# Attention units in rounds of five with borrowed PSUM banks, and queries loaded two chunks ahead

## The chip, the cores and the metric

The kernel runs on one core of a Trainium2 chip. The metric is the device time of one execution in microseconds (us), the median over runs. Engines are named as the profile names them: PE multiplies matrices (PEld loads its weights), DVE and ACT work on vectors, POOL is the general engine, SP issues most of the DMAs.

## What is computed

The reference normalises an input of 2048 tokens by 512 features and adds two branches to it. The first is differential attention: 16 heads, each with two softmax maps of depth 16 over one 32-wide value, causal; the difference of the two maps is filtered along the tokens (an FFT with a Gaussian), normalised and projected. The second is a mixture of experts: every token goes through a shared expert and through the best 2 of 8 routed experts.

```python
s = einsum('bthd,bshd->bhts', q, k) * scale
a = softmax(where(causal, s, NEG))          # for q1,k1 and for q2,k2
o = concat([a @ v1, a @ v2])
attn = irfft((rfft(attn1) - lambda_full * rfft(attn2)) * filt) # then rms norm, @ Wout
y = sum_k topk_w[k] * expert_k(x) + shared(x)
out = x + attn_branch(layernorm(x)) + ffn_branch(layernorm(x))
```

## The kernel before, in words

Three stages follow each other: a beginning (normalise, route, project queries and keys, store them in DRAM), the function `middle` (attention and experts interleaved), and `ending` (filter, output projection, and the gathering of the experts' rows). The change is in `middle`, which holds PE from 254.0 us to about 1221 us of the profiled execution.

The attention is cut into 32 **chunks**: 8 groups `g` of two heads, and in each group four blocks of 512 queries, `qc` = 3, 2, 1, 0. A chunk is a list of **units** (`Chunk.units`). A unit is one head and one block of 128 keys (`kb`): both softmax maps of that head against 512 queries. Units on the diagonal are narrower, and two of them share one; these are called masked. A chunk has 8 qc + 5 units, so there are 68 in a group and 544 in all. `LEAD` says how many whole key blocks come ahead of the diagonal.

`scores` (L831) works a unit off: two matmuls side by side, each on 64 rows of the array (maps s = 0 and 1), into the two halves of a PSUM tile `ps_s`; ACT takes the exponential of both halves in one instruction (L844) into `pt`; POOL zeroes the masked triangles (L853). Later `values` (L875) multiplies `pt` with the values, four matmuls side by side of 32 columns, into `ps_o`; DVE adds `pt` up into `sum` (L889, L892), which `sums` (L901) and `finish` (L913 to L930) turn into the divisor.

PSUM has eight banks here. `sc_ps` has 2 tiles of two banks, `av_ps` one bank, and `f_ps` three banks, handed out by `bank`, which the experts' products use (`wh` L244, `wy` L283, `ps_x` L167, `xh` and `xg` L181, `ps_u` L204, `xy` L214), and the chunk's ends too (`ps_sum`, `ps_ot`, `ps_st`).

The order of the work on PE is written out in the main loop at the end of `middle`, one **round** for every four units of the stream: scores of the first two units; the value products that are pending (`todo`), and the sums of a chunk that ended in the round before (`closing`); scores of the other two units; the remaining value products; then `work()`, one or more pieces of the experts, until their share of the work done has caught up with the share of the stream. `added` puts DVE's sums between the pieces. At the end of a round POOL may get up to two steps of `folded`, which prepares the filter for a finished group.

When a chunk's first unit comes up, `burst` issues loads on SP's queue: `load_queries` of the next chunk (8 DMAs of 64 KB, two buffers for each head), and `load_keys` of the next group for the block of keys that this group has done with (4 DMAs of 128 KB). The experts' weights go over the same queue (`fetch`, L151: 704 or 768 KB each), issued by the pieces of the experts as buffers come free. Six of the last eight of the 34 routed tiles hold two experts of 64 tokens each, and fetch two sets of weights for a tile.

Of the kernel before, what the change touches and what calls it, by code (L numbers as in the profile page):

```python
# [8 lines left out]
F32 = mybir.dt.float32  # L9
F32R = mybir.dt.float32r  # L10
BF16 = mybir.dt.bfloat16
I32 = mybir.dt.int32
AF = mybir.ActivationFunctionType
# [57 lines left out]
def block_kernel(  # L71
# [521 lines left out]
    def middle(general):  # L593


        with ExitStack() as pools:
# [130 lines left out]

            def load_keys(g, c):
                for h in (2 * g, 2 * g + 1):
                    k = kp.tile([P, QC], F32R, tag=f"k{c}", name="kS", bufs=4 if c == 0 else 2)  # L730
                    for s in range(2):
                        src = parts[1][2 * h + s, :, :, c * QC : (c + 1) * QC].rearrange("a d t -> (a d) t")
                        nc.sync.dma_start(
                            k[64 * s : 64 * s + 64, :].bitcast(F32),
                            src.unsqueeze(0).to_broadcast([2, 2 * D, QC]),
                        )
                    keys[h, c] = k

            def load_queries(g, qc):
                for h in (2 * g, 2 * g + 1):  # L740
                    q = qp.tile([P, QC], F32R, tag=f"q{h % 2}", name="qS")
                    for s in range(2):
                        for rep in range(2):
                            r = 64 * s + 32 * rep
                            nc.sync.dma_start(
                                q[r : r + 32, :].bitcast(F32),
                                parts[0][2 * h + s, rep : rep + 2, :, qc * QC : (qc + 1) * QC].rearrange("a d t -> (a d) t"),
                            )
                    queries[h, qc] = q
# [45 lines left out]
            def masked(chunk, unit):  # L795
                return any(kb >= chunk.qc * TQ for _, kb, *_ in unit)

            class Chunk:
# [6 lines left out]
                def units(self):  # L805


                    d = self.qc * TQ
                    for kb in [*range(LEAD[self.qc]), d]:
                        for h in range(2):  # L810
                            yield [(h, kb, 0, 0, QC)]
                    for h in range(2):
                        yield [(h, d + 1, P, 0, 3 * P), (h, d + 3, 3 * P, 3 * P, P)]
                    last = [(h, d + 2, 2 * P, 2 * P * h, 2 * P) for h in range(2)]
                    yield from ([part] for part in last) if general else [last]
                    for kb in range(LEAD[self.qc], d):
                        for h in range(2):
                            yield [(h, kb, 0, 0, QC)]

                def scores(self, unit):  # L820

                    g, qc = self.g, self.qc
                    if general and not self.probs:
                        self.shift = greatest(g, qc)
                    ps = sps.tile([P, 2, QC], F32, tag="sc", name="ps_s")
                    for h, kb, off, col, w in unit:
                        for s in range(2):
                            r = slice(64 * s, 64 * s + 64)
                            k = keys[2 * g + h, kb // TQ][r, kb % TQ * P : (kb % TQ + 1) * P]
                            to = ps[:, s, col : col + w]  # L830
                            nc.tensor.matmul(  # L831
                                to, k, queries[2 * g + h, qc][r, off : off + w], start=True, stop=not general
                            )
                            if general:
                                r = 64 * h + 32 * s
                                nc.tensor.matmul(
                                    to, ones[r : r + 1, :], self.shift[r : r + 1, off : off + w],
                                    start=False, stop=kb < qc * TQ,
                                )
                                if kb >= qc * TQ:  # L840
                                    nc.tensor.matmul(to[:, :P], identb, mask, start=False, stop=True)
                    pt = pp.tile([P, 2, QC], F32, tag="pt", name="pt")
                    used = slice(min(c for *_, c, _ in unit), max(c + w for *_, c, w in unit))
                    nc.scalar.activation(pt[:, :, used], ps[:, :, used], AF.Exp, scale=SCALE)  # L844
                    if masked(self, unit) and not general:

                        cols = [col for *_, col, _ in unit]
                        if cols == [0, 2 * P]:
                            chosen = [pt.rearrange("p s (h q) -> p (s h) q", h=2)[:, :, :P]]
                        else:  # L850
                            chosen = [pt[:, :, col : col + P] for col in cols]
                        for part in chosen:
                            nc.gpsimd.affine_select(  # L853
                                out=part, in_=part, pattern=[[0, part.shape[1]], [1, P]], compare_op=ALU.is_ge,
                                fill=0.0, base=0, channel_multiplier=-1,
                            )
                    ready = []
                    for h, kb, off, col, w in unit:
                        self.probs[h, kb] = pt[:, :, col : col + w], off
                        if (1 - h, kb) in self.probs:  # L860
                            ready.append((self, kb))
                    return ready
# [133 lines left out]
            ex = experts()  # L996
            for c in range(NQC):
                load_keys(0, c)
                if c == 0:
                    load_queries(0, NQC - 1)  # L1000
            worked, begun, summed, held = 0.0, -1, 0, []
            todo, closing, closed, shared, ready, folding = [], [], [], [], [], None

            def burst(units):
                nonlocal begun
                found = []
                for n, chunk, unit in units:
                    if n > begun:
                        begun = n
                        if n + 1 < len(turns):  # L1010
                            load_queries(*turns[n + 1])

                        if chunk.g + 1 < NG:
                            load_keys(chunk.g + 1, (chunk.qc + 1) % NQC)
                    found += chunk.scores(unit)
                return found

            def values():
# [16 lines left out]
                    else:  # L1035
                        held.append((n, c, unit))

            for i in range(0, len(stream), 4):
                units = stream[i : i + 4]
                found = burst(units[:2])  # L1040
                n, ended = values()
                for c in closing:
                    c.sums()
                    summed += 1
                if n < 2 and not closing:

                    work()
                found += burst(units[2:])
                while todo:
                    ended += values()[1]  # L1050
                todo += found
                for c in closed:
                    c.put(nc.gpsimd)
                    if c.qc == 0:
                        ready.append(c.g)
                closed, closing = closing, ended
                for c in closed:
                    c.finish()
                held, before = [], held
                added(before)  # L1060
                added(units[:2])
                later = [u for u in units[2:] if not masked(*u[1:])]
                while True:
                    work()
                    added(later[:1])
                    later = later[1:]
                    if worked / (work_all - left) >= (i + 4) / len(stream):
                        break
                added(later)
                added(u for u in units[2:] if masked(*u[1:]))  # L1070
                if any(masked(*u[1:]) for u in units) or not shared:
                    steps = 0
                elif any(masked(*u[1:]) for u in stream[i + 4 : i + 8]):
                    steps = 1 if ready or units[0][1].g == NG - 1 else 0
                else:
                    steps = 2
                for _ in range(steps):
                    if folding is None and ready:
                        folding = folded(ready.pop(0), nc.gpsimd)
                    if folding is not None and next(folding, 0) == 0:  # L1080
                        folding = None
# [401 lines left out]
```

## Time and profile before

| what | value |
|---|---|
| median of 3 runs | 1334.18 us (1333.29 to 1334.27) |
| profiled execution, its own time | 1336.14 us |
| its span, first to last instruction | 1334.3 us |
| PE busy | 1305.5 us, 98% of the span |
| DVE, ACT, POOL busy | 1007.7, 690.5, 620.3 us |
| scores L831, matmuls and busy | 1280, 204.5 us |
| values L875, matmuls and busy | 2560, 267.7 us |
| exponentials L844 | 544, 1022 ns each |
| granted PE clock, mean | 0.996 |

A row of the timeline gives the start of a group of equal instructions, how long it lasted, the engine, the line, what is written from what, rows by columns of the array, and how many there were; square brackets show idle time of the engine ahead of it and what ended it. The lasting of matmuls overlaps, so differences of starts are what counts. An fp32 product takes two matmuls of the trace where the program has one.

### The profile page before, as it was taken

How to read it: one execution, taken by the hardware profiler on the slowest of the kernel's cores; microseconds unless marked ns; L12 is line 12 of the kernel's file. 1: busy time of each engine (PE TensorE's matmuls, PEld its weight loads, DVE VectorE, ACT ScalarE, POOL GpSimd, SP SyncE). 2: the span in 40 equal slices, each digit the busy share in tenths (PEclk: the TensorE clock that was granted, in tenths of full speed). 3: DMA queues.
4: the chain of work that ended last, by engine and by line, in shares of the span. 5: the costliest groups of instructions: out<-in, count | busy, mean ns of one | idle time of the engine just before them, and what ended most of it. 6: DMA issues, size and time to landing. Idle time of an engine off the chain costs nothing.

```text
span 1334.3 us, 20914 instructions
## 1 busy us (share of the span) xinstructions
PE 1305.5 (98%) x7554; PEld 598.5 (45%) x7554; DVE 1007.7 (76%) x1316; ACT 690.5 (52%) x848; POOL 620.3 (46%) x639
## 2 busy tenths in 40 slices
PE   7999999999999999999999999999999999999998
PEld 3444444434343444444445444444544443445544
DVE  7049883277777868778987988888798869876784
ACT  2311110265666566666666666666666657662231
POOL 0002331012131233215985976894598666741774
PEclk9999999999999999999999999999999999999999
DMA  9405773201210023235566666566666667878998
GB/s 371 184 16 163 201 205 102 89 16 32 66 63 22 29 78 93 77 111 160 169 186 202 183 196 188 149 215 191 170 199 189 191 186 271 314 266 304 190 222 188
DMA packets 82058, 215.07 MB, mean 161 GB/s; under 512 B 12964, under 2 KB 13416, under 8 KB 81688
## 3 DMA queue, kind: packets, MB, share of 16 engines
q1 hardware_dynamic: 69224, 186.47, 43.9%
q0 software_dynamic: 11056, 22.78, 8.7%
q10 hardware_dynamic: 1664, 4.38, 1.0%
q8 instruction: 63, 1.03, 0.4%
q14 instruction: 51, 0.42, 0.1%
HBM read 170.48 MB, written 43.10 MB: 160 GB/s over the span
## 4 chain that ended last, share of the span: by engine, by line
PE 64%; POOL 8%; DMA 5%; issue 2%; DVE 2%; ACT 0%; SPq 0%; POOLq 0%; DVEq 0%; ACTq 0%
PE ps_o L875 17%; PE ps_s L831 12%; PE wh L244 8%; PE xy L214 6%; PE xh L181 5%; PE xg L181 5%; PE wy L283 4%; POOL res L1138 3%; DMA res<-ysh 2%; PE ps_sum L901 2%; DMA w<-in_wex_dram 1%; PE ps_x L167 1%; POOL pt L853 1%; DVE sum L892 1%; PE ps_ot L913 1%
## 5 line engine op out<-in xcount | busy, mean ns | idle before, releaser
L892 DVE TENSOR_TENSOR sum<-sum,pt 128x1024 f32<-128x1024 f32 (+2 forms) x576 | 628.7, 1140 | 30.4 <-POOL pt L853 13.6
L844 ACT ACTIVATE pt<-ps_s 128x1024 f32<-128x1024 f32 x544 | 527.3, 1022 | 182.5 <-PE ps_s L831 127.3
L853 POOL TENSOR_SCALAR_AFFINE_SELECT pt<-pt 128x256 f32<-128x256 f32 (+1 forms) x224 | 164.4, 756 | 368.4 <-ACT pt L844 342.9
L875 PE MATMUL ps_o<-pt,vd 128*32 128x512 f32 (+3 forms) x2560 | 267.7, 534 | 1.9 <-POOL pt L853 1.9
L831 PE MATMUL ps_s<-qS,kS 64*128 64x512 f32 (+3 forms) x1280 | 204.5, 407 | 1.6 <-DVEq L1346 1.2
L831 PEld LDWEIGHTS ps_s<-qS,kS 64*128 64x128 f32 x1280 | 97.5, 185 | 177.3 <-issue 96.7
L244 PE MATMUL wh<-xnT,w 128*128 128x512 f32 (+1 forms) x352 | 150.4, 574 | 0.0
L875 PEld LDWEIGHTS ps_o<-pt,vd 128*32 128x32 f32 x2560 | 67.2, 109 | 123.3 <-issue 105.9
L495 POOL DMA_INDIRECT who<-pairs,slot x32 | 33.8, 1055 | 171.3 <-DVE pairs L492 104.3
L542 PE MATMUL ps_x<-xnT,wqk_sb 128*128 128x512 f32 x256 | 110.5, 593 | 0.0
L244 PEld LDWEIGHTS wh<-xnT,w 128*128 128x128 f32 x352 | 64.1, 190 | 72.6 <-issue 56.5
L214 PE MATMUL xy<-w,uT 128*128 128x512 f32 (+3 forms) x240 | 94.6, 599 | 1.2 <-DVE rcp L916 1.2
L181 PE MATMUL xh<-w,xT 128*128 128x352 f32 (+1 forms) x320 | 90.4, 477 | 4.0 <-DMA w<-in_wex_dram 3.2
L181 PE MATMUL xg<-w,xT 128*128 128x352 f32 (+1 forms) x320 | 88.6, 468 | 0.0
L930 POOL TENSOR_TENSOR vd<-o_n 128x128 f32<-128x128 f32 x60 | 58.1, 986 | 53.8 <-DVE o_n L921 53.7
L542 PEld LDWEIGHTS ps_x<-xnT,wqk_sb 128*128 128x128 f32 x256 | 48.4, 190 | 60.6 <-issue 60.6
L283 PE MATMUL wy<-w,ws 128*128 128x512 f32 x160 | 74.8, 603 | 0.0
L559 ACT CAST hi<-turned 128x1024 fp32r<-128x1024 f32 x16 | 16.7, 1045 | 93.9 <-DVE turned L557 59.3
L1138 POOL DMA_INDIRECT res<-ys,slot x32 | 53.3, 1667 | 23.7 <-DMA res<-ysh 11.7
L181 PEld LDWEIGHTS xh<-w,xT 128*128 128x128 f32 (+1 forms) x320 | 48.3, 178 | 31.0 <-issue 9.3
L181 PEld LDWEIGHTS xg<-w,xT 128*128 128x128 f32 (+1 forms) x320 | 46.6, 174 | 34.4 <-issue 14.8
L377 PE MATMUL ps_tv<-wv_sb,xnT 128*128 128x512 f32 x128 | 59.8, 620 | 0.7 <-ACT xnT L374 0.7
(252 smaller groups left out, 1368.4 us busy)
## 6 DMA issues: line engine op xcount, KB each, us to landing
w<-in_wex_dram SPq DMA_DIRECT2D x88, 704.0 KB
w<-in_wex_dram SPq DMA_DIRECT2D x44, 768.0 KB
kS<-parts_k SPq DMA_DIRECT2D x128, 128.0 KB
qS<-parts_q SPq DMA_DIRECT2D x256, 64.0 KB
ys<-y_sb SPq DMA_DIRECT2D x34, 256.0 KB
parts_q<-hi SPq DMA_DIRECT2D x32, 256.0 KB
parts_k<-hi SPq DMA_DIRECT2D x16, 256.0 KB
parts_k<-turned SPq DMA_DIRECT2D x16, 256.0 KB
```

Source lines behind the costliest of these rows:

```text
L181: nc.tensor.matmul(dst[r, :], xT[:, c, r], w[:, c * FI : (c + 1) * FI], start=(c == 0), stop=(c == NE - 1), skip_group_check=True,)
L214: nc.tensor.matmul(y[r, :], uT[:m, ic, r], w[:m, ic * E : (ic + 1) * E], start=(ic == 0), stop=(ic == NF - 1), skip_group_check=True,)
L244: nc.tensor.matmul(dst, w_sb[o // WUP][o % WUP // WONE][:, o % WONE : o % WONE + P], x[:, c, :], start=(c == 0), stop=(c == NE - 1),)
L283: nc.tensor.matmul(y, us[i][:, t * P : (t + 1) * P], w_sb[i // NF][2][:, i % NF * E : (i % NF + 1) * E], start=(i == 0), stop=(i == SCH - 1),)
L377: nc.tensor.matmul(pv, xnT[:, c, t * P : (t + 1) * P], wv_sb[:, c, :], start=(c == 0), stop=(c == NE - 1))
L542: nc.tensor.matmul(ps[:, i, :], wqk_sb[st, qk][:, i, c, :], xnT[:, c, cols], start=(c == 0), stop=(c == NE - 1),)
L831: nc.tensor.matmul(to, k, queries[2 * g + h, qc][r, off : off + w], start=True, stop=not general)
L844: nc.scalar.activation(pt[:, :, used], ps[:, :, used], AF.Exp, scale=SCALE)
L853: nc.gpsimd.affine_select(out=part, in_=part, pattern=[[0, part.shape[1]], [1, P]], compare_op=ALU.is_ge, fill=0.0, base=0, channel_multip ...
L875: nc.tensor.matmul(self.o[r : r + 32, off:], vd[:, kb, v0 : v0 + 32], pt[:, s, :], start=first, stop=self.ended, skip_group_check=True,)
L892: nc.vector.tensor_add(to, to, pt)
L1138: nc.gpsimd.indirect_dma_start(out=came[k], out_offset=None, in_=ys, in_offset=bass.IndirectOffsetOnAxis(ap=slot[:, step - 2, order[k] : o ...
```

## The change

- A round takes 5 units where no chunk ended in the round before (`closing` is empty), else 4. The second burst of such a round has three units, and the first of them (`apart`) puts its scores in two banks from `f_ps` (`ps_a`) in the place of a `ps_s` tile. Its exponential is two instructions of 512 columns.
- Queries have three buffers for each head, and are loaded two chunks ahead: `load_queries(*turns[n + 2])`, and the first two chunks' before the loop, the second of them between the keys of block 1 and block 2.
- The keys of block 0 have two buffers, not four. They are loaded when their own group begins, not a group ahead; so the chunk `qc` = 3 takes its key blocks 4 to 15 first and 0 to 3 last.
- POOL's steps of `folded` in a round: one if the round's units hold no masked one, one more if the next four hold none.

```diff
-                    k = kp.tile([P, QC], F32R, tag=f"k{c}", name="kS", bufs=4 if c == 0 else 2)
+                    k = kp.tile([P, QC], F32R, tag=f"k{c}", name="kS")
...
-                    q = qp.tile([P, QC], F32R, tag=f"q{h % 2}", name="qS")
+                    q = qp.tile([P, QC], F32R, tag=f"q{h % 2}", name="qS", bufs=3)
...
-                    for kb in [*range(LEAD[self.qc]), d]:
+                    kbs = [*range(TQ, d), *range(TQ)] if self.qc == NQC - 1 else [*range(d)]
+                    for kb in [*kbs[: LEAD[self.qc]], d]:
...
-                    for kb in range(LEAD[self.qc], d):
+                    for kb in kbs[LEAD[self.qc] :]:
...
-                def scores(self, unit):
+                def scores(self, unit, apart):
...
-                    ps = sps.tile([P, 2, QC], F32, tag="sc", name="ps_s")
+                    if apart:
+                        banks = [bank([P, QC], "ps_a") for _ in range(2)]
+                    else:
+                        ps = sps.tile([P, 2, QC], F32, tag="sc", name="ps_s")
+                        banks = [ps[:, s] for s in range(2)]
...
-                            to = ps[:, s, col : col + w]
+                            to = banks[s][:, col : col + w]
...
-                    nc.scalar.activation(pt[:, :, used], ps[:, :, used], AF.Exp, scale=SCALE)
+                    if apart:
+                        for s in range(2):
+                            nc.scalar.activation(pt[:, s, used], banks[s][:, used], AF.Exp, scale=SCALE)
+                    else:
+                        nc.scalar.activation(pt[:, :, used], ps[:, :, used], AF.Exp, scale=SCALE)
...
-                if c == 0:
-                    load_queries(0, NQC - 1)
+                if c < 2:
+                    load_queries(0, NQC - 1 - c)
...
-                        if n + 1 < len(turns):
-                            load_queries(*turns[n + 1])
-
-                        if chunk.g + 1 < NG:
-                            load_keys(chunk.g + 1, (chunk.qc + 1) % NQC)
-                    found += chunk.scores(unit)
+                        if n + 2 < len(turns):
+                            load_queries(*turns[n + 2])
+
+                        c = (chunk.qc + 1) % NQC
+                        g = chunk.g + (c > 0)
+                        if 0 < g < NG:
+                            load_keys(g, c)
+                    found += chunk.scores(unit, k == len(units) - 3)
...
-            for i in range(0, len(stream), 4):
-                units = stream[i : i + 4]
+            upto = 0
+            while upto < len(stream):
+
+                many = 4 if general or closing else 5
+                units = stream[upto : upto + many]
+                upto += many
...
-                    if worked / (work_all - left) >= (i + 4) / len(stream):
+                    if worked / (work_all - left) >= upto / len(stream):
...
-                if any(masked(*u[1:]) for u in units) or not shared:
-                    steps = 0
-                elif any(masked(*u[1:]) for u in stream[i + 4 : i + 8]):
-                    steps = 1 if ready or units[0][1].g == NG - 1 else 0
-                else:
-                    steps = 2
-                for _ in range(steps):
+                steps = [
+                    shared and not any(masked(*u[1:]) for u in some) for some in (units, stream[upto : upto + 4])
+                ]
+                for _ in range(sum(map(bool, steps))):
```

## Prediction

> **What bounds the kernel now.** I read the page's busy shares and its chain first.
>
> ```profile
> PE 1305.5 (98%) x7554; PEld 598.5 (45%) x7554; DVE 1007.7 (76%) x1316; ACT 690.5 (52%) x848; POOL 620.3 (46%) x639
> PE 64%; POOL 8%; DMA 5%; issue 2%; DVE 2%; ACT 0%; SPq 0%; POOLq 0%; DVEq 0%; ACTq 0%
> ```
>
> PE is the bound of the span and, in `middle`, of nearly every stretch; the POOL and DMA shares of the chain lie mostly after 1221 us, in the ending, which the change doesn't edit and which starts when `middle` is done. So time can be won in `middle` only if PE needs less of it, or waits less. No matmul goes away. The timeline of PE shows what can: how long a group holds PE depends on what is beside it.
>
> ```profile
> 242.32 4.45 PE L283 MATMUL wy<-w,ws 128*128 128x512 f32 x10
> ...
> 246.61 1.02 PE L283 MATMUL wy<-w,u_last 128*128 128x512 f32 x2
> ...
> 415.71 3.70 PE L244 MATMUL wh<-xnT,w 128*128 128x512 f32 x8
> 419.34 0.73 PE L831 MATMUL ps_s<-qS,kS 64*128 64x512 f32 x4
> 420.00 1.92 PE L875 MATMUL ps_o<-pt,vd 128*32 128x512 f32 x16
> 421.85 0.73 PE L831 MATMUL ps_s<-qS,kS 64*128 64x512 f32 x4
> 422.52 2.84 PE L244 MATMUL wh<-xnT,w 128*128 128x512 f32 x6
> ```
>
> From start to start, ten full-array matmuls in an unbroken run take 246.61 - 242.32 = 4.29 us, 0.429 each. Eight of them between scores take 419.34 - 415.71 = 3.63 us, where 8 x 0.429 = 3.43: **0.20 us of switching for each stay in the experts' form**. Sixteen value matmuls, four side by side, take 421.85 - 420.00 = 1.85, where 4 x 0.429 = 1.72: 0.138 us (unrounded starts) for each stay in the values' form. Two units of scores cost 0.66 after either. In the starts of single matmuls the 0.20 splits into 0.105 on the way in and 0.093 on the way out, the 0.138 into 0.024 and 0.114. These repeat to a few ns over the whole stage.
>
> Then PE's waits and what was behind the largest:
>
> ```profile
> PE xh L181 <- DMA w<-in_wex_dram: 3.2, 2, 2.1
> PE ps_o L875 <- POOL pt L853: 1.9, 3, 1.4
> PE xy L214 <- DVE rcp L916: 1.2, 1, 1.2
> ```
>
> SP's queue, and PE at the wait:
>
> ```profile
> 1068.75 7.43 SPq L745 DMA_DIRECT2D qS<-parts_q  x8
> 1076.22 2.38 SPq L733 DMA_DIRECT2D kS<-parts_k  x4
> 1079.99 3.89 SPq L151 DMA_DIRECT2D w<-in_wex_dram  x4
> ```
>
> ```profile
> 1094.84 0.78 PE L181 MATMUL xh<-w,xT 128*64 128x352 f32 x2 [2.08 <-DMA w<-in_wex_dram]
> 1096.69 4.96 PE L181 MATMUL xh<-w,xT 128*64 128x352 f32 x14 [1.07 <-DMA w<-in_wex_dram]
> ```
>
> And the stretch after it (PE, PEld, DVE, ACT and POOL busy with counts, PE clock, DMA share, GB/s):
>
> ```profile
> 1095.00:1103.00 8.00, 6.93 (x24) 2.36 (x27) 2.67 (x5) 1.03 (x2) 5.15 (x5) 0.57 0.50 140
> ```
>
> At 1092 us PE waits for the second two-expert tile's weights, which stood behind a chunk's loads on SP. After it the granted clock is 0.57 over 1095 to 1103 (the trace has half clock for 6.83 us). The episode costs 2.08 + 1.07 us idle and half of 6.83: 6.5 us. Such waits in `middle` sum to about 14 us, this one the largest.
>
> **The change part by part.** *Rounds of five.* I counted stays in the order of PE's instructions in both built programs, from the first score to the last value product: 84 rounds of five and 31 of four in place of 136 of four; stays in the experts' form (128 rows, transposes of a chunk's end included) 155 before, 127 after; stays in the values' form 153 before, 134 after. So 28 x 0.198 + 19 x 0.138 = 5.5 + 2.6 = **8.2 us less on PE**. The third unit in a burst costs what a unit costs: start to start the pairs of scores take 0.32 to 0.33 us in either place. The switch costs lie on the path, as PE has no slack here; from below the saving is bounded at nothing, if each switch removed is found again as a wait.
>
> By the Trainium skill, page "TensorEngine Tiling (Array Packing)", section "Key Properties", a change of tiling mode drains the array; "TensorE: Matmul & The Clock Gate", section "Part 2", in "Single matmul latency", puts a drain at about 175 ns. Two switches for each of the 47 stays would then be an estimate of 16 us, or 1318; the starts above show 24 to 114 ns a switch, so the measurement decides.
>
> *The borrowed banks.* The third unit no longer waits for the first's exponential. What is new: two of the three expert banks are held until ACT has read them. Take a round as in the timeline, from its first score at 0: values end at 2.5, the three units at 3.5. ACT does a 1024-column exponential every 0.92 us (row: 1022 ns, overlapping), so the first two end at 2.4, the borrowed two at about 3.5 and 4.0, the last two by 5.9. The expert's first product starts at 3.5 in the third bank; its second, where a round has a short product first (`ps_u` or `ps_x`, 0.48 us), at 4.0 in the first borrowed bank: ready by half a microsecond. The next round's first two scores come no earlier than 3.5 + 2.56 = 6.1 and 6.4, and want the tiles free at 5.0 and 5.9: covered, but by 0.5 us for the second. Splitting an exponential costs ACT between 0.04 (at the 0.48 us pitch of its 512-column copies) and 0.26 us (two unoverlapped 592 ns instructions) a round: at most 22 us, on an engine that is free for 640. I take 0 for PE, and as the other end 0.1 us in each of 84 rounds, 8.4 us.
>
> *Masks on POOL.* A round of five may hold a whole diagonal: seven selections at 0.76 us. Before, the widest selection of each chunk ended 0.56 to 5.9 us ahead of its value product, median 3.6; the distance on PE between that score and that product is 5.2 to 8.6 us before and 5.3 to 11.3 after. Steps of `folded` ahead of masked rounds stay one or two of some 5 us. No leftover step is at the end. I take 0; the ends are -1.9 (the row's waits gone) and +4.
>
> *The loads.* Query and key loads keep their number and size, at the same chunk starts. At the start, eight query loads come ahead of the keys of blocks 2 and 3. SP took from 215.5 to 227.3 for eight, so the last keys go out near 258 and land near 264; the first unit that wants them stands in the third round, after 254 + 19 = 273. Hidden, with 9 us to spare. Late, the last group's first chunk now brings four key loads (0.5 MB) that the kernel before had sent a group earlier; they stand behind the weights of the second two-expert tile and ahead of that tile's successor. The earlier queries take a risk away: the eight that SP reached at 1083.9 took 16.7 us to go out, and now have a chunk more of time. For the wait at 1092 itself: after, the loads of chunk (6, 0) stand one weight fetch further ahead of the tile's, but the distance on PE from that chunk's start to the tile, summed from the rows' durations along each built order, is 21.5 us, where it was 21.4. So I take the episode as unchanged; the ends are -6.5 (gone) and +6.5 for each further one.
>
> By the page "TensorE: Matmul & The Clock Gate", section "Why this matters for your kernels", idle gaps under some 3 us keep the clock. The row above speaks against it: the longest gap before the half clock was 2.08 us. By the rule that part, 3.4 us, would not be there to lose.
>
> **Sum.** The profiled execution took 1336.14 for a span of 1334.3, and 1336.14 - 8.2 = 1327.9. It stands 2.0 above the median of 1334.18; taken off the median, 8.2 gives **1326.0**.
>
> **Rivals.** *A, the weights come in time:* the fetch of the second double tile is behind fewer bytes in flight. 8.2 + 6.5 less: 1319.5. For it, DMA was only 18% busy at 1075 to 1080 while SP stood in front of its query slots; against it, the equal distance.
>
> *B, the saving is eaten in small waits:* 0.1 us for banks in each round of five, 8.4 us, or masks at 0.26 us in each of 32 chunks. 1334. For it, covers of half a microsecond; against it, scores started later than their usual distance by under 3 us in all of the 136 rounds.
>
> *C, slower:* one mechanism, weights late on SP in the stretch of double tiles (1070 to 1200 us), each time with the half clock after it. Price 6.5 us each; two more than now give 1334.2 - 8.2 + 13 = 1339. It makes the kernel slower from 1.7 of them on ((8.2 + 2.7) / 6.5). For it, DMA at 0.8 to 0.9 there and 0.5 MB of keys added; against it, only one in the six double tiles before.
>
> *D, it doesn't do what it says* is out: the built order shows the rounds and stays counted above.
>
> **How the numbers follow.** Forecast 52% (1322.5 to 1329.5 of its own: POOL and the smaller waits -3.5 to +3.5), A 20%, B 16%, C 12%. About 0.2%, 2.7 us, is what a measurement of this kernel can tell from no change. Faster: forecast, A and a third of B that ends below 1331.5, 0.77; same: the rest of B, 0.11; slower: 0.12. The range leaves out C and A's best: 1317 to 1334.
>
> **What would show it.** PE's timeline should show scores in groups of six, value groups of 24, and stays still 0.20 and 0.138 us over their matmuls; PE busy near 1297. Wrong if PE's idle list gains `ps_a`, `xh` or `xy` behind ACT, or `ps_o` behind POOL, over 3 us; if the clock shows a second half-clock stretch; or none, which is A.

## The result and the profile after

The changed kernel takes **1407.64 us** (median of 4, 1405.58 to 1408.99) beside 1333.74 us for the kernel before (median of 4): a ratio of 1.0553, with a 95% interval of 1.0534 to 1.0571. It is slower by 5.5%, where 1326.0 was forecast. The profiled execution took 1407.89 us for a span of 1406.2, against 1336.14 and 1334.3 before; its mean granted clock is 0.971, against 0.996.

The first view is again the page of the changed kernel: its busy shares, the row of the granted PE clock in 40 slices (in tenths, 9 is 90% or more), and the chain by engine.

```profile
PE 1315.9 (94%) x7554; PEld 612.5 (44%) x7554; DVE 1011.3 (72%) x1316; ACT 694.5 (49%) x932; POOL 615.8 (44%) x639
...
PEclk9999999999899999999998999799889989999999
...
PE 56%; DMA 11%; POOL 9%; issue 3%; DVE 2%; SPq 1%; ACT 1%; POOLq 0%; DVEq 0%; ACTq 0%
```

PE has the same 7554 instructions and is busy 10 us longer, not 8 us shorter. Its share of the chain has gone from 64% to 56%, and DMA's from 5% to 11%. The clock has dips at regular distances. The kernel before had none in its row:

```profile
PEclk9999999999999999999999999999999999999999
```

PE's waits in the changed kernel (waiting tile and line, releaser, us in total, times, longest):

```profile
PE ps_s L838 <- DMA kS<-parts_k: 51.0, 16, 6.4
...
PE ps_s L838 <- issue: 6.7, 2, 3.7
PE xh L181 <- DVE rcp L927: 2.6, 1, 2.6
...
PE ps_u L204 <- DVE xtanh L198: 1.8, 1, 1.8
...
PE xy L214 <- DMA w<-in_wex_dram: 1.6, 1, 1.6
PE ps_o L886 <- POOL pt L864: 1.4, 4, 0.5
PE ps_a L838 <- DMA kS<-parts_k: 1.3, 1, 1.3
```

The first row is new and is the result: scores wait 51 us for **keys**, and the "issue" row (6.7) is of the same places, as the timeline below shows. The wait for weights that the prediction dwelt on is 1.6 us here. The seven places are the starts of groups 1 to 7: by the starts of the trace 10.3 us at 366, 3.9 at 500, 1.6 at 617, 7.2 at 740, 13.1 at 872, 13.0 at 1007 and 10.5 at 1143 us, 59.7 together before rounding.

One of them in full. SP's queue around the sixth, in the changed kernel:

```profile
988.75 12.19 SPq L151 DMA_DIRECT2D w<-in_wex_dram  x3
1000.98 7.75 SPq L745 DMA_DIRECT2D qS<-parts_q  x8
1008.78 2.27 SPq L733 DMA_DIRECT2D kS<-parts_k  x4
...
1013.08 12.59 SPq L745 DMA_DIRECT2D qS<-parts_q  x8
```

PE there, and the stretch as a whole (busy PE, PEld, DVE, ACT and POOL with counts, PE clock, DMA share, GB/s):

```profile
1004.53 2.74 PE L214 MATMUL xy<-w,uT 128*128 128x512 f32 x6
1013.69 0.76 PE L838 MATMUL ps_s<-qS,kS 64*128 64x512 f32 x1 [6.42 <-DMA kS<-parts_k]
1016.35 0.79 PE L838 MATMUL ps_s<-qS,kS 64*128 64x512 f32 x1 [1.89 <-DMA kS<-parts_k]
1020.09 0.76 PE L838 MATMUL ps_s<-qS,kS 64*128 64x512 f32 x1 [2.95 <-issue]
1022.64 0.79 PE L838 MATMUL ps_s<-qS,kS 64*128 64x512 f32 x1 [1.79 <-DMA kS<-parts_k]
1023.36 4.18 PE L886 MATMUL ps_o<-pt,vd 128*32 128x512 f32 x32
```

```profile
1007.00:1027.00 20.00, 6.95 (x33) 2.52 (x36) 4.27 (x6) 2.79 (x4) 3.93 (x5) 0.58 0.41 115
```

The four key loads leave SP at 1008.78, behind eight query loads that took 7.75 us to go out; PE has stood since 1007.3. It gets one matmul per landed load until 1022.6. Which keys are they? Of the **next** group, block 1 (`kb` 4 to 7). They are issued when the chunk `qc` = 0 begins, five units ahead of the next group. In the kernel before, the chunk `qc` = 3 began with `kb` 0 to 3, whose keys had been loaded a group earlier, and wanted `kb` 4 with its 9th unit. The changed one begins with `kb` 4, so that the same load, issued at the same point, is wanted eight units sooner. Around it the clock is 0.58: after the seven stops the trace records 78.5 us at half clock (13.65, 3.41, 3.41, 10.24, 17.07, 17.07 and 13.65), and in all of `middle` 81.9: another 3.41 follow the 2.6 us that `xh` waits behind `rcp`.

**A ledger.** The starts of the trace allow a sum for `middle`. Each stay of PE in one form lasts from its first start to the next stay's first start; take off its matmuls at their unbroken pace, and the median of what is left is the price of a stay. What stands over 0.15 us above that price is a wait or half clock. Kernel before: 17.7 us of such excess; changed kernel: 105.6. The stays became fewer, 106.5 us before and 89.8 now. So 87.9 - 16.7 = 71.2 us more, against 71.9 between the two spans. The forecast failed by the first number; the second is twice what it gave.

### The profile page after: what moved, and what is told of

It reads as the page before. It is cut to its first block, busy times and chain, and to the rows that moved or that the text cites. A ratio compares the mean times of both kernels' runs of the same rounds, so it can differ in the third digit from the quotient of the medians.

```text
span 1406.2 us, 20962 instructions
## 1 busy us (share of the span) xinstructions
PE 1315.9 (94%) x7554; PEld 612.5 (44%) x7554; DVE 1011.3 (72%) x1316; ACT 694.5 (49%) x932; POOL 615.8 (44%) x639
## 4 chain that ended last, share of the span: by engine, by line
PE 56%; DMA 11%; POOL 9%; issue 3%; DVE 2%; SPq 1%; ACT 1%; POOLq 0%; DVEq 0%; ACTq 0%
PE ps_o L886 15%; PE ps_s L838 8%; PE wh L244 8%; DMA kS<-parts_k 6%; PE xh L181 5%; PE xy L214 5%; PE xg L181 5%; PE wy L283 3%; POOL res L1152 2%; PE ps_a L838 2%; DMA w<-in_wex_dram 2%; PE ps_sum L912 2%; DMA res<-ysh 2%; POOL pt L864 2%; PE ps_ot L924 1%
## 5 line engine op out<-in xcount | busy, mean ns | idle before, releaser
L855 ACT ACTIVATE pt<-ps_s 128x1024 f32<-128x1024 f32 x460 | 447.3, 1028 | 169.2 <-PE ps_s L838 130.3
L864 POOL TENSOR_SCALAR_AFFINE_SELECT pt<-pt 128x256 f32<-128x256 f32 (+1 forms) x224 | 183.5, 845 | 353.7 <-ACT pt L855 272.1
L886 PE MATMUL ps_o<-pt,vd 128*32 128x512 f32 (+3 forms) x2560 | 270.8, 546 | 1.5 <-POOL pt L864 1.4
L838 PE MATMUL ps_s<-qS,kS 64*128 64x512 f32 (+3 forms) x1082 | 174.9, 396 | 59.7 <-DMA kS<-parts_k 51.0
L838 PEld LDWEIGHTS ps_s<-qS,kS 64*128 64x128 f32 x1082 | 90.5, 186 | 151.1 <-issue 106.5
L853 ACT ACTIVATE pt<-ps_a 128x512 f32<-128x512 f32 x168 | 91.6, 596 | 54.5 <-PE ps_a L838 37.6
L941 POOL TENSOR_TENSOR vd<-o_n 128x128 f32<-128x128 f32 x60 | 49.7, 848 | 136.7 <-DVE o_n L932 136.7
L927 DVE RECIPROCAL rcp<-ps_st 128x16 f32<-128x16 f32 x32 | 8.2, 255 | 106.7 <-PE ps_st L925 106.7
```

Of the source, the lines that this page charges most:

```text
L838: nc.tensor.matmul(to, k, queries[2 * g + h, qc][r, off : off + w], start=True, stop=not general)
L853: nc.scalar.activation(pt[:, s, used], banks[s][:, used], AF.Exp, scale=SCALE)
L864: nc.gpsimd.affine_select(out=part, in_=part, pattern=[[0, part.shape[1]], [1, P]], compare_op=ALU.is_ge, fill=0.0, base=0, channel_multip ...
L886: nc.tensor.matmul(self.o[r : r + 32, off:], vd[:, kb, v0 : v0 + 32], pt[:, s, :], start=first, stop=self.ended, skip_group_check=True,)
```

## The experiments

Theory K: the order of the key blocks makes the first scores of groups 1 to 7 wait for loads; nothing else in the change costs much. Rivals: the rounds of five, which use keys up faster (F), and the loads' traffic, whose effect is on the weights (L). The "excess" given with each run is the ledger's, for its `middle`.

**a_order: the changed kernel with the key blocks 8 to 11 first.** These are loaded two chunks ahead of the group; `kb` 4 is again wanted with the 9th unit.

```diff
-  kbs = [*range(TQ, d), *range(TQ)] if self.qc == NQC - 1 else [*range(d)]
+  kbs = [*range(2 * TQ, d), *range(TQ, 2 * TQ), *range(TQ)] if self.qc == NQC - 1 else [*range(d)]
```

> The changed kernel with one line other: the chunk qc = 3 takes key blocks 8 to 11, then 4 to 7, then 0 to 3 (with its lead of six and the diagonal as before), in the place of 4 to 11, then 0 to 3. Theory (keys too late): the loss is that block 1's keys go out when chunk (g, 0) begins, five units ahead of the chunk that now starts with them; here they are wanted eight whole units later, so the waits of scores on kS (about 60 us in the changed kernel) fall under 3 us, the half-clock stretches at the groups' beginnings go, and the time is that of the 8.2 us saved: 1326 (1320 to 1332). Rival 1 (queue overfull: two chunks of queries ahead, and block 0's keys at a group's start, make all keys late): waits on kS stay over 30 us, 1370 to 1410. Rival 2 (rounds of five themselves stall PE): 1370 to 1410 with waits on ACT.

Measured: 1339.04 us (8 runs), ratio 1.0027 (1.0017 to 1.0038); clock 0.992, excess 33.8. Its largest waits of PE in `middle`:

```profile
PE xy L214 <- DMA w<-in_wex_dram: 7.9, 1, 7.9
...
PE xh L181 <- DMA w<-in_wex_dram: 3.1, 2, 2.2
PE xh L181 <- DVE rcp L927: 3.1, 2, 2.6
PE xh L181 <- ACT xT L169: 2.5, 1, 2.5
```

Scores wait for no keys any more: one line gives 69 of the 74 us back. But the time lies above the range of K (1320 to 1332), as the kernel is not the 8 us faster that was forecast. A wait for weights of 7.9 us with 10.24 us at half clock has come, and waits of 2.5, 1.8 and 2.65 us at 597, 612 and 742 us.

**b_order: the kernel before with the changed order of key blocks alone.**

```diff
-  for kb in [*range(LEAD[self.qc]), d]:
+  kbs = [*range(TQ, d), *range(TQ)] if self.qc == NQC - 1 else [*range(d)]
+  for kb in [*kbs[: LEAD[self.qc]], d]:
...
-  for kb in range(LEAD[self.qc], d):
+  for kb in kbs[LEAD[self.qc] :]:
```

> The kernel before with the changed kernel's order of key blocks in chunk qc = 3 alone (4 to 11, then 0 to 3); rounds of four, loads, buffers as before. Theory (keys too late): the whole loss and nothing of the gain: waits on kS of about 60 us, half clock for about 80 us in all, 1334 + 75 to 85, so 1409 to 1419. Rival 1 (queue overfull): no loss without the other loads, 1334. Rival 2 (rounds of five): 1334.

Measured: 1417.22 us, ratio 1.0603 (1.0584 to 1.0622); clock 0.970, excess 100.5. The first waits of PE:

```profile
PE ps_s L832 <- DMA kS<-parts_k: 44.2, 17, 4.7
PE ps_s L832 <- issue: 9.5, 4, 3.0
PE ps_s L832 <- DMA w<-in_wex_dram: 7.6, 2, 4.1
```

All three rows are scores of the first units of a group. Three lines in the kernel before, without rounds of five and without queries two chunks ahead, cost 82 us. So the order of the key blocks is the cause, shown from both sides; whether the rest of the change is free, the other half of K, is asked further down.

**a_four: the changed kernel with rounds of four.**

```diff
-  found += chunk.scores(unit, k == len(units) - 3)
+  found += chunk.scores(unit, False)
...
-  many = 4 if general or closing else 5
+  many = 4
```

> The changed kernel with rounds of four throughout, so without the borrowed banks; order of keys, loads and buffers as changed. Theory (keys too late): the loss without the gain, 1405 to 1420. Rival 1 (queue overfull): the same, 1405 to 1420. Rival 2 (rounds of five): 1334.

Measured: 1424.47 us, ratio 1.0660 (1.0642 to 1.0677); excess 109.5. It lies 4 us above K's range. Without the rounds of five the kernel is 17 us slower still: F is out as the cause, and the rounds are worth about twice the forecast's 8.2.

**b_five: the kernel before with the rounds of five alone**, banks and split exponential as in the change, loads and key order as before.

```diff
-  for i in range(0, len(stream), 4):
-      units = stream[i : i + 4]
+  upto = 0
+  while upto < len(stream):
+      many = 4 if general or closing else 5
+      units = stream[upto : upto + many]
+      upto += many
...
+  if apart:
+      banks = [bank([P, QC], "ps_a") for _ in range(2)]
```

> The kernel before with rounds of five and the borrowed banks alone; order of key blocks, loads, buffers and the rule for POOL's steps as before. Theory (keys too late; the rounds save what was counted): 1334 - 8 = 1326, scores never waiting for kS. Rival 1: 1326 as well. Rival 2 (rounds of five stall PE): 1370 to 1410. Of the prediction's own rivals: if banks or masks eat the saving, 1334.

Measured: 1334.09 us (10 runs), ratio 0.9987 (0.9977 to 0.9997); excess 31.0. The 1326 of the expectation did not come. The saving on the stays is there and nearly eaten, by the same waits at 597, 611 and 741 us, by 4.5 us for weights at 1089, and by 1.9 us for queries and 1.2 for keys at 956. The time is that of the rival "banks or masks", but none of these waits is for a borrowed bank or a mask. The one at 741 us is for another bank: `xh` reads only weights and ACT's copy `xT`, so what it waits for behind DVE's `rcp` can only be its bank of `f_ps`, which a chunk's end (`ps_st`) holds until then.

**a_keys: the changed kernel with the key loads issued ahead of the queries'.** A smaller dose of the same delay.

```diff
+  c = (chunk.qc + 1) % NQC
+  g = chunk.g + (c > 0)
+  if 0 < g < NG:
+      load_keys(g, c)
   if n + 2 < len(turns):
       load_queries(*turns[n + 2])
-
-  c = (chunk.qc + 1) % NQC
-  g = chunk.g + (c > 0)
-  if 0 < g < NG:
-      load_keys(g, c)
```

> The changed kernel with each chunk's key loads put ahead of its query loads on SP; order of key blocks as changed (4 to 11 first). Theory (keys too late, by the time from issue to first use): SP took 7.75 us for the eight query loads in front of the keys at 1001 us, so each group's wait on kS shrinks by about that. The seven groups' waits were 10.3, 3.9, 1.6, 7.2, 13.1, 13.0 and 10.5 us; less 7.75 each, not below 0, they leave 16 of 60 us. With less half clock: 1345 to 1370. Rival (total traffic makes keys late, wherever they stand): as changed, 1400 to 1412.

Measured: 1368.59 us in one run only (before: 1334.83, median of 17), excess 64.7; the waits for keys are 20.2 us in place of 51.0. The place in SP's queue is more than half of the cost; five units are too short for the loads even without the queries ahead.

**a_both: both, the order of a_order and the queue of a_keys.**

> The changed kernel with both edits: key blocks 8 to 11, 4 to 7, 0 to 3 in chunk qc = 3, and each chunk's keys loaded ahead of its queries. Theory: keys were in time already with the order alone, so this does what the order alone does, 1336 to 1341 beside 1335 before; the 7.9 us wait for a weight of the experts at 1104 us stays, since as many loads stand ahead of that weight on SP. Rival (keys that are only just in time hold small waits): 1330 or less.

Measured: 1332.94 us (10 runs), ratio 0.9984 (0.9973 to 0.9994), excess 30.0: below the theory's range and above the rival's, so neither had it. The wait for weights near 1101 us stays, with 5.5 us and 6.83 us at half clock. Which load is ahead of which among a chunk's own does not free the weights.

**a_order4: a_order with rounds of four** (the edit of a_four). It asks whether that wait is brought by the rounds or by the loads.

> The kernel with the mended order (8 to 11, 4 to 7, 0 to 3) and the changed loads, in rounds of four. It tells what ate the 8.2 us in the mended order. Theory L (the loads: block 0's keys now go out at the group's start, and hold the weights of the double tiles up on SP): the 7.9 us wait with its half clock stays, 1343 to 1350. Theory R (the rounds of five are what brings the new waits, on weights too): 1333 to 1337, no wait for a weight over 3 us.

Measured: 1355.69 us, ratio 1.0156 (1.0141 to 1.0171), excess 34.5; it is above L's range (1343 to 1350). Its waits of PE on experts' operands:

```profile
PE xy L214 <- DMA w<-in_wex_dram: 6.7, 1, 6.7
PE xy L214 <- DVE rcp L927: 4.9, 2, 3.1
PE xh L181 <- DMA w<-in_wex_dram: 4.1, 2, 3.0
```

The weights are late with rounds of four too, so L holds for that part: the changed loads delay them. The waits of 2.5 and 1.8 us at 597 and 611 are gone (0.7 is left for the copy), so those belong to the rounds of five. The pair a_order and a_order4 gives the rounds' worth again: 15.8 us between the profiled executions (1336.91 and 1352.74); L's range was too low since it went by 8.2. And the second half of K falls: with the keys in time and rounds of four, the rest of the change still costs 21 us beside the kernel before.

What L means can be read from SP's queue in a_order. The wait on PE was from 1103.7 to 1111.59.

```profile
1078.17 14.63 SPq L745 DMA_DIRECT2D qS<-parts_q  x8
1092.84 2.37 SPq L733 DMA_DIRECT2D kS<-parts_k  x4
...
1097.04 4.51 SPq L151 DMA_DIRECT2D w<-in_wex_dram  x5
```

The chunks `qc` = 0 and the next `qc` = 3 begin only five units apart, and each sends eight query loads and four key loads. The second's queries took 14.63 us to leave SP, and the five weight loads behind them went out from 1097.04 on. But neither those queries (wanted two chunks on) nor the keys of block 0 (now wanted last) are urgent.

**a_late: a_both, where a chunk `qc` = 3 of a later group sends its key loads with its 7th unit and its query loads with its 13th.**

```diff
-  if n > begun:
-      begun = n
+  late = chunk.qc == NQC - 1 and chunk.g > 0 and not general
+  seen[n] = seen.get(n, 0) + 1
   c = (chunk.qc + 1) % NQC
   g = chunk.g + (c > 0)
-  if 0 < g < NG:
+  if seen[n] == (7 if late else 1) and 0 < g < NG:
       load_keys(g, c)
-  if n + 2 < len(turns):
+  if seen[n] == (13 if late else 1) and n + 2 < len(turns):
       load_queries(*turns[n + 2])
```

> The mended order, rounds of five, and loads spread out: keys ahead of queries, and in chunk qc = 3 the keys of block 0 at its 7th unit and the queries at its 13th, not at its first, so that the weights of the second double tile stand ahead of them on SP. Theory L: the wait of 7.9 us for weights goes, with about 5 us of half clock after it; from the 1339 of the mended order, 1326 (1324 to 1331), faster than the kernel before. Theory R: 1336 to 1340.

Measured: **1327.86 us** (6 runs), ratio 0.9947 (0.9931 to 0.9963). It beats both kernels. Excess 23.5, mean clock 0.997. SP's queue at the same place:

```profile
1075.11 4.51 SPq L151 DMA_DIRECT2D w<-in_wex_dram  x5
...
1081.07 9.69 SPq L733 DMA_DIRECT2D kS<-parts_k  x4
1092.10 3.50 SPq L151 DMA_DIRECT2D w<-in_wex_dram  x4
1095.64 16.92 SPq L745 DMA_DIRECT2D qS<-parts_q  x8
```

The weights now go out at 1075, ahead of the keys, and at 1092, between keys and queries, and no wait for them is longer than 0.9 us.

**a_late4: a_late with rounds of four.** The rounds' worth, when no load is late.

> The kernel with the mended order and the loads moved to the 7th and 13th unit (1327.9 us), with rounds of four units again: it isolates the rounds of five once no load is late. Theory S (a stay in the scores' form costs 0.20 us as one in the experts' form does, so that the rounds of five save 16.7 us of PE, of which the waits they bring at 597, 611 and 741 us, 7 us with no 3.41 us of half clock, give a part back): 1336 to 1343 us, PE busy near 1306. Theory P (the prediction's sum, 8.2 us, third unit of a burst at the price of a unit): 1330 to 1335 us. If the waits for the weights near 1100 us come back although the loads of keys are spread, the time lies above 1343 and the loads, not the rounds, decide.

Measured: 1347.68 us (4 runs, 1343.75 to 1352.11), ratio 1.0107 (1.0088 to 1.0126). Both theories' ranges were missed, S by less; its own bound said that above 1343 the loads would decide, but its waits for weights are 3.5 us where the kernel before has 3.2. PE's row of the page, of a_late4 first and then of a_late:

```profile
PE 1306.9 (97%) x7554; PEld 597.5 (45%) x7554; DVE 1009.8 (75%) x1316; ACT 690.5 (51%) x848; POOL 597.8 (45%) x639
```

```profile
PE 1289.4 (97%) x7554; PEld 602.7 (45%) x7554; DVE 1011.5 (76%) x1316; ACT 692.9 (52%) x932; POOL 617.7 (47%) x639
```

PE is busy 17.5 us less with rounds of five, as S had it (near 1306); the profiled executions are 15.4 us apart (1343.75 and 1328.34). The profiled run of a_late4 is the fastest of its four, and the trace can't say what the others, up to 8.4 us longer, did. That stays open.

Beside the kernel before, a_late4 is 13.1 us longer by the medians and 7.6 by the profiled executions, so what the change does apart from the rounds is not free even with the loads spread. Part of it is on record: `xy` waits 4.9 us behind `rcp`, where the kernel before has 1.2. Ahead of the longest of these waits, 3.14 us at 795, DVE stood 3.69 us for a mask that POOL began only at 790.12, after steps of `folded`. The new rule for these steps was never run by itself, so that it is the reason is not shown.

**a_late_xt: a_late, where the first routed tile's copies get a round of attention units.**

```diff
-  yield 0.6
+  yield 4.0
...
-  if late:
-      yield 3.2
+  yield 3.2
```

> The same kernel with the first routed tile's copies given a round of attention units: the pause after its transposes as long as a round, and the pause ahead of its gate's tanh kept also for the first tile. Theory W (the waits of 2.5 us at 597 and of 1.83 us at 611, with the 3.41 us at half clock behind the first, are lost time): both waits go and the time is 1321 to 1325 us. Rival (the units spent there are missing later, so that the wait moves to another tile or to the end of the loop): within 1.5 us of 1327.9 with the same sum of waits at other places.

Measured: 1334.27 us (11 runs), ratio 0.9997 (0.9987 to 1.0006). The waits at 597 and 611 went, as W said (at 597 scores now wait 1.1 us for an exponential), and the time rose by 6 us. So W's price is refuted, and the rival is right in kind and not in size: the units spent there are missing at the end of the loop. PE in a_late_xt, at that end:

```profile
1194.32 0.27 PE L924 MATMUL ps_st<-cst,s_sb 128*128 128x128 f32 x1
1197.79 0.80 PE L244 MATMUL wh<-kept,w 128*128 128x128 f32 x2 [3.19 <-DMA w<-in_wex_dram]
```

In a_late the attention's last products run until 1196.5 us, and the same `wh` starts at 1199.78 without a wait; here they are used up by 1191.4, PE waits 3.19 us, and 3.41 us at half clock follow. Another 2.65 us wait with half clock behind it is in the ending, at 1287.

## Why the prediction was wrong

**The bound: right.** PE bounds `middle`, before and after; no gain came from anything but stays and waits.

**The loads: the step that failed.** The prediction says "Query and key loads keep their number and size, at the same chunk starts" and concludes "Hidden" (the part *The loads*). Number, size and starts were right. What moved was the point where the loaded keys are wanted, from the 9th unit of the next group to the first. I worked the distance out for the very first loads of the program (9 us to spare) and for the weights' tile at 1092, and not for the other key loads, which are sent five units before their group. b_order shows it without the rest of the change (ratio 1.0603), a_order by undoing it (1.0027). The price that was missing is seven stops with 59.7 us of waiting, and matmuls at half clock around them: PE busy 1315.9 against 1289.4 in a_late, which has the same instructions and stays, 26.5 us.

**Rounds of five: right in sign, half in size.** The second step that failed is a term of the sum. I gave 8.2 us; the stays give 16.7. The timeline of a_late, undisturbed, shows the term that I left out.

```profile
408.18 2.78 PE L886 MATMUL ps_o<-pt,vd 128*32 128x512 f32 x24
410.89 0.50 PE L838 MATMUL ps_a<-qS,kS 64*128 64x512 f32 x2
411.23 0.63 PE L838 MATMUL ps_s<-qS,kS 64*128 64x512 f32 x4
411.79 3.70 PE L244 MATMUL wh<-xnT,w 128*128 128x512 f32 x8
415.42 0.73 PE L838 MATMUL ps_s<-qS,kS 64*128 64x512 f32 x4
416.08 1.92 PE L886 MATMUL ps_o<-pt,vd 128*32 128x512 f32 x16
```

Three units take 411.79 - 410.89 = 0.90 us (0.895 unrounded), two take 416.08 - 415.42 = 0.66 (0.663). So the third costs 0.232, not the "0.32 to 0.33" that I had from the pairs' starts: 2 x 0.232 is 0.463, and the 0.20 that remain are the price of a stay in the scores' form, the same as in the experts'. There are 272 such stays before and 230 after, which is 42 x 0.20 = 8.4 us; with 28 x 0.198 and 19 x 0.138 it makes 16.6, and the ledger's medians give 16.7. The experts' and the values' price were right: 24 value matmuls take 410.89 - 408.18 = 2.71, where 6 x 0.429 = 2.57. The page "TensorEngine Tiling (Array Packing)" of the Trainium skill, section "Key Properties", with the latency that the prediction cites, came to an estimate of 16 us there. That this meets the 16.7 is chance: the estimate took 47 stays at 0.35 us, and the runs show 89 fewer (28 + 19 + 42) at 0.14 to 0.20.

**Where the 16.7 went, once the order is mended.** a_order's excess is 16.1 us above that of the kernel before (33.8 - 17.7), and so it gains nothing. In a_late the excess is 5.8 above it, which leaves 10.9 in `middle`, 7.3 over the whole span. Where the last 3.6 went was not followed up.

**Borrowed banks and masks: right with rounds of five, near 0.** PE's waits on the split exponential are 0.8 and 0.3 us in all in the changed kernel and 0.3 in b_five, a_order and a_late; `ps_o` waits 1.4 us for POOL in place of 1.9. With rounds of four masks did cost something, by way of DVE, as a_late4 shows.

**What no step had** are three waits of routed tiles that come in this size with rounds of five: for ACT's copy `xT` (2.5 us at 597), for DVE's product `xtanh` (1.8 at 611), and for the bank that a chunk's end holds until `rcp` (2.65 at 741). In the kernel before, PE waits 0.7 us for the first, not for the second, and 1.2 at another place behind `rcp`. A round of attention between the copy and its product removes the first two, as a_late_xt shows, but takes it from a later place.

**The rivals.** A (the weights in time, 1319.5) and B (small waits) did not come. C had the side and the mechanism of the smaller part: weights late on SP behind a chunk's loads, with half clock after them, hold a_order back: a_late, where they are gone, is 11 us faster. That a_order's 1339.04 meets C's 1339 is chance. C set 13 us for two more such waits against a saving of 8.2; a_order has one longer wait and the three just named, against a saving of 16.7. The changed kernel itself is slower by another mechanism, one that repeats with every group, and for which the range had no term.

## What to carry to other kernels

When a change reorders what consumes a buffer, write down for every load, not for the first ones only, when it is issued, what is ahead of it in its queue, and which instruction wants it first; the load need not move to become late. A late load costs more than its wait where the clock falls after it. And when fewer switches between forms are what a change wins, count the stays in every form: the difference between runs of two lengths gives the price of an element, and what it leaves over is the price of the stay.

## What the runs showed of the hardware

**The clock falls by windows, not by the length of a gap.** All inner stretches at half clock, in every trace here, are multiples of 3.413 us long, and within one trace they begin on one grid of 3.413 us. Laying that grid over all twelve traces, and counting the windows that were at full clock: each one in which PE stood for 1.91 us or more was followed by half clock (43 of 43); of those with 1.69 to 1.83 us, two of eight were; of those with less, none. A window already at half clock needs less: from 0.80 us on, every one was followed by another. A gap that lies across two windows can be spared. In a_late4 the longest gap, on PE and in the clock of its stretch (the third figure from the right):

```profile
794.05 0.60 PE L167 MATMUL ps_x<-cst,xrow 128*128 128x128 f32 x4
797.79 2.42 PE L214 MATMUL xy<-w,uT 128*128 128x512 f32 x5 [3.14 <-DVE rcp L927]
```

```profile
793.00:800.00 7.00, 3.86 (x18) 2.11 (x17) 6.72 (x8) 2.61 (x4) 5.46 (x8) 1.00 0.84 308
```

And in a_late a shorter one, with the stretch after it:

```profile
596.09 0.65 PE L167 MATMUL ps_x<-cst,xrow 128*128 128x128 f32 x4
599.24 1.54 PE L181 MATMUL xh<-w,xT 128*128 128x352 f32 x2 [2.50 <-ACT xT L169]
```

```profile
599.00:602.30 3.30, 3.06 (x5) 1.85 (x6) 0.00 (x0) 0.19 (x1) 0.74 (x1) 0.50 0.74 174
```

A gap of 3.14 us leaves the clock at 1.00, since the grid parts it into 1.69 and 1.45; one of 2.50 halves it, since 2.21 of it lie in one window. The Trainium skill, page "TensorE: Matmul & The Clock Gate", section "Part 1: The HAM clock gate (the "warmup" mystery)", has such a free-running window of 3413 ns, and lets the clock fall after an idle one. The windows agree with these traces; but one that is idle for 1.91 us of its 3.41 is enough here.

**A row of query loads holds SP.** Eight 64 KB loads took 7.75, 12.59 and 14.63 us to leave its queue in the rows above, and whatever stands behind them, keys or weights, goes out later by as much. Where the keys stand in the queue was worth about 39 us here (a_keys, a single run, against the changed kernel).
